# A state space layer in one fused kernel: projection split so that times and angles come first, functions on ScalarE put in order, one scaling moved from GpSimd to ScalarE

## The chip, the cores and the metric

The kernel runs on one core of a Trainium2 chip. A core has five engines that run side by side, each working through its own queue in order: PE (TensorE, matrix products into the PSUM memory), DVE (VectorE, elementwise work and sums along a row), ACT (ScalarE, functions such as exp, tanh, sine, one instruction at a time with a table of functions loaded), POOL (GpSimd, elementwise work from SBUF and scatters by index) and SP (SyncE, which here issues the transfers). The metric is device time in microseconds of a whole execution; smaller is better.

## The reference

Four sequences of 512 tokens, 128 numbers each, go through four layers. Each layer's result is added to its input and the sum is normalised.

1. Attention in a band of 64 tokens to either side, 16 heads.
2. A mixture of experts: 12 experts, of which each token takes the best two, plus one shared expert.
3. A state space layer, cut here to what the change touches:

```python
proj = u @ W_in                                   # 684 columns
z, x, Bp, Cp, dd_dt, dd_A, trap_raw, angles = jnp.split(proj, idx, axis=-1)   # 256 256 64 64 4 4 4 32
Bp = _layernorm(Bp, Bn_g, Bn_b);  Cp = _layernorm(Cp, Cn_g, Cn_b)
DT = jax.nn.softplus(dd_dt + dt_bias)
phase = jnp.cumsum(angles * DT.mean(-1, keepdims=True), axis=1)
Bp_rot, Cp_rot = _rope_pairs(Bp, phase), _rope_pairs(Cp, phase)     # turned by cos and sin of phase
A = jnp.minimum(-jax.nn.softplus(dd_A), -A_FLOOR)
decay = jnp.exp(A * DT);  trap = jax.nn.sigmoid(trap_raw)
# h = decay * h + (trap * x B + (1 - trap) * previous x B) * DT ;  y = h C      step by step
y = (y + D_param * x4) * jax.nn.silu(z4)
out = y @ W_out
```

4. A second mixture of experts: 8 experts of width 512, the best two, each expert's result normalised before it is weighted.

## The kernel before

Tokens lie on the 128 partitions, in four blocks per sequence. The program has three parts.

The first (lines 1698 to 1703) is attention, then routing and the first experts. Tokens are scattered by POOL into a table in main memory, one stretch per expert; tiles of 128 rows are loaded, multiplied, and scattered back (`ys_a`). The third (1716 to 1725) does the same for the second experts. In both, each engine's queue has the order in which the program is written (`as_written`).

The change lies in the second part, lines 1706 to 1715. Two generators `pair(0)` and `pair(1)`, for two sequences each, are traced in turns: pair 0 alone for 40 us of the costs that stand in its `yield` statements, then the two side by side, whichever has had less cost first (`side_by_side`). Within a pair `together` takes one step of each of several generators in turn. Here the order on each engine is not the order of tracing: the framework's planner plays the program through at compile time with durations of its own; an engine takes, of the instructions that are ready in this play, the one traced first. The queue so made is then fixed, and on the chip an instruction that waits holds up all behind it on its engine.

One pair goes through these steps, all in `ssm` (1494):

- `moe0_back` (1058): loads the two results of each token's two experts (`back`, two buffers, on SP's queue), and `combine` (1042) weights them. POOL multiplies the first result by its weight (1046) and adds the shared expert's output (1047); DVE adds the second (1051) and takes mean and variance. `layernorm` then takes a root on ACT (299) and normalises on ACT (312).
- `ssm_project` (1119): transposes the rows on PE and copies them to SBUF on ACT (290, 293). For each of 8 blocks it multiplies by the last 428 columns of the weights (1132) and ACT copies the result to `pj` (1135). Then the first 256 columns, the gate `z`, are projected in transposed form (1141), ACT takes the tanh (1144), and DVE makes `zt` (1147).
- `ssm_norm` (1150) and `ssm_weights` (1178), together. The first squares B and C on ACT (1156), sums on DVE (1159), takes a root on ACT, multiplies on DVE (1165) and applies gain and bias on POOL (1173, four operations). The second works on the 44 columns of times and angles: bias (1187), tanh and exp (1194, 1196), logarithm (1203), a row of small DVE steps to `vals` (1205 to 1227), a shift by one token and a prefix sum on PE (1233 to 1250), range reduction on DVE (1258 to 1264), three sums for decays on PE (1269), sine and cosine (1275, 1277) and exp (1282, 1285) on ACT. The decays are stored as rows in main memory (1308) so that `chunk_load` (1367) can load them spread over the partitions.
- `ssm_turn` (1311): turns B and C by sine and cosine on DVE and POOL (1324, 1325, 1330), transposes them (1342), and forms their products (1359, 1362).
- For each of four blocks, `chunk_matrix` (1385) makes the decay matrix by a scan on DVE (1395) and a product on POOL (1414), and the scaled x on POOL and ACT (1403, 1409). `chunk_outputs` (1424) forms the state and the outputs on PE (1432, 1441, 1447, 1454) and multiplies by `zt` (1472). `chunk_out` (1477) projects out and adds the residual. After two blocks follow the layer norm and the routing for the second experts: gates on DVE, ranks on PE (425), scatters on POOL (467).

Six PSUM banks (`bank`) go round for all products of this part. The tiles `nrm` and the decay matrices share two SBUF buffers (tag `b`).

Of the kernel before, what the change touches and what calls it, by code (L numbers as in the profile page):

```python
# [9 lines left out]
F32 = mybir.dt.float32  # L10
BF16 = mybir.dt.bfloat16
I32 = mybir.dt.int32
AF = mybir.ActivationFunctionType
# [3 lines left out]
P = 128  # L17
# [12 lines left out]
NPROJ = 684  # L30
# [9 lines left out]
class Kernel:  # L40
# [34 lines left out]
    @contextmanager  # L75
    def as_written(self, *engines):

        e = mybir.EngineType
        kinds = {"PE": e.PE, "ACT": e.Activation, "DVE": e.DVE, "POOL": e.Pool, "SP": e.SP}
        last = self.nc.cur_bb.bb.instructions[-1]  # L80
        yield
        traced = self.nc.cur_bb.bb.instructions
        first = next(i for i in reversed(range(len(traced))) if traced[i] is last) + 1
        before = {kinds[k]: [] for k in engines}
        puts = {}
        order = mybir.DependencyInfo(mybir.DependencyClass.NoSync, mybir.DependencyReason.DATA)
        for i in traced[first:]:
            if i.engine in before:
                put = i.name in self.put_names
                for name in before[i.engine] + ([] if put else puts.get(i.engine, [])):  # L90
                    self.tc.add_manual_dep(i, name, order, reason="as written")

                if put:
                    puts.setdefault(i.engine, []).append(i.name)
                else:
                    before[i.engine], puts[i.engine] = [i.name], []

# [944 lines left out]
    def combine(self, y, back, w, mv):  # L1042
# [3 lines left out]
        nc.gpsimd.tensor_tensor(first, first, w[:, 0, :, None].to_broadcast([P, NT, D]), ALU.mult)  # L1046
        nc.gpsimd.tensor_tensor(first, first, y, ALU.add)
        yield 2.6
# [70 lines left out]
    def ssm_project(self, h, x, s):  # L1119


        nc = self.nc
        n = NPROJ - DI
        xt = [self.transposed([x[k][:, i, :] for i in range(NT)], f"xt2_{h}{k}") for k in range(HB)]
        pj = s["pj"] = self.sp.tile([P, HC, n], F32, tag="pj", name=f"pj{h}")
        zt = s["zt"] = self.sp.tile([P, 2, HB, T], F32, tag="zt", name=f"zt{h}")
        yield 1.2
        yield 0.5
        for i in range(NT):
            for k in range(HB):  # L1130
                pp = self.bank(f"ppj{h}_{i}_{k}")
                nc.tensor.matmul(
                    pp[:, :n], lhsT=xt[k][:, i * P : (i + 1) * P], rhs=self.w_in[:, DI:], start=True, stop=True
                )
                nc.scalar.copy(pj[:, i * HB + k, :], pp[:, :n])
            yield 1.6
        for k in range(HB):
            pz = [self.bank(f"pz{h}_{k}_{c}") for c in range(2)]
            tz = [self.s2.tile([P, T], F32, tag="a", name=f"tz{h}_{k}_{c}", bufs=9) for c in range(2)]
            for c in range(2):  # L1140
# [3 lines left out]
                nc.scalar.activation(tz[c], pz[c], AF.Tanh, scale=0.5)  # L1144
# [33 lines left out]
    def ssm_weights(self, h, s):  # L1178

        nc, n = self.nc, HC  # L1180
        o = DI + 2 * NS
        pj = s["pj"]
# [5 lines left out]
            v, pj[:, :, o : o + 8], self.dtb[:, None, :].to_broadcast([P, n, 8]), ALU.add  # L1188
# [5 lines left out]
        nc.scalar.activation(tr, pj[:, :, o + 8 : o + 12], AF.Tanh, scale=0.5)  # L1194
# [33 lines left out]
            vals.rearrange("p (c k) -> p c k", c=n), pj[:, :, o + 12 : o + 44],  # L1228
# [39 lines left out]
        for k, lhsT in enumerate((self.gt, self.ones, self.lt)):  # L1268
# [6 lines left out]
        nc.scalar.activation(sn.rearrange("p c k -> p (c k)"), r, AF.Sin)  # L1275
        cs = self.s2.tile([P, n, 32], F32, tag="c", name=f"cs{h}", bufs=5)
        nc.scalar.activation(
            cs.rearrange("p c k -> p (c k)"), ph, AF.Sin, bias=self.half_pi, scale=-1.0
        )
        s["turn"] = sn, cs  # L1280
        dec = small([P, 4, n, NH1], "dec")
        nc.scalar.activation(
            dec[:, :3].rearrange("p k i h -> p (k i h)"), pd[:, : 3 * m], AF.Exp
        )
        nc.scalar.activation(dec[:, 3], ash, AF.Exp)
# [208 lines left out]
    def ssm(self, h, first, behind):  # L1494
# [5 lines left out]
        yield from self.ssm_project(h, x, s)  # L1500
        yield from self.together([self.ssm_norm(h, s), self.ssm_weights(h, s)])
        for i in range(2):
            self.chunk_load(h, i, s)
        yield from self.ssm_turn(h, s)
# [271 lines left out]
```

## Time and profile before

| | |
|---|---|
| Median of 3 runs | 702.22 us (702.03 to 704.40) |
| The profiled execution, device time | 701.83 us |
| Its span in the trace | 700.1 us |
| Busy: PE, weight load, DVE, ACT, POOL | 510.5, 372.4, 424.2, 307.2, 358.7 us |
| Last scatter of the first experts issued | 373.22 us |
| First loaded rows weighted (line 1046) | 381.63 us |
| First weights step of pair 0 (line 1187) | 404.85 us |
| Sine of pair 0, of pair 1 (line 1275) | 428.44, 473.23 us |
| First scan of pair 0 (line 1395) | 435.92 us |
| First bias copy of the second experts (line 546) | 570.97 us |

How to read the profile: times are us from the start of the span, and the span is some 1.7 us shorter than the device time. A line of the timeline gives start, length, engine, line, operation, output<-input with partitions x elements, and in brackets how long the engine sat idle before and what ended the wait. "PEld" is the load of a stationary operand. A float32 product appears as two matmul passes. An average over the span says little here, since its parts have different limits; the stretches are read one by one.

### The profile page before, as it was taken

Reading aid. Unit: us, or ns where it says so; the run is one execution under the profiler, and the core shown is the slowest. Engines: PE = TensorE matmul, PEld = TensorE weight load, DVE = VectorE, ACT = ScalarE, POOL = GpSimd, SP = SyncE. Lnnn points to the kernel's source line nnn. Section 1 sums busy time; section 2 is a strip of 40 time slices with the busy share of each in tenths; the row PEclk is TensorE's granted clock in tenths of the full one; section 3 lists DMA queues with packets and bytes.
Section 4 is the critical chain, followed back from the end, with each engine's and each line's share of the span. In section 5 each row is a group of like instructions: output and inputs, shape, how many; then the busy total and the mean of one; then the engine's idle time right before and its main releaser. Section 6 shows DMA issues by size and latency. Waiting matters only on the chain.

```text
span 700.1 us, 13358 instructions
## 1 busy us (share of the span) xinstructions
PE 510.5 (73%) x4232; PEld 372.4 (53%) x4232; DVE 424.2 (61%) x1412; ACT 307.2 (44%) x799; POOL 358.7 (51%) x509
## 2 busy tenths in 40 slices
PE   6899789688886985999992618673675569898800
PEld 2344344254443644999992306363464459888700
DVE  5565656756734361566662666999774535777745
ACT  2154554454462420455551474914423317566525
POOL 9254324723847041455554322667864655888831
PEclk9799999979978696899997676766676559999955
DMA  6999999998000004688876202113110135766442
GB/s 177 220 158 154 160 157 155 154 143 125 32 2 31 1 23 143 176 249 250 256 220 183 74 0 84 46 38 107 45 47 16 46 84 156 187 179 179 125 133 60
DMA packets 93936, 83.63 MB, mean 119 GB/s; under 512 B 8869, under 2 KB 78650, under 8 KB 93866
## 3 DMA queue, kind: packets, MB, share of 16 engines
q1 hardware_dynamic: 88554, 71.85, 48.0%
q0 software_dynamic: 5312, 10.92, 5.3%
q8 instruction: 35, 0.57, 0.3%
q14 instruction: 35, 0.29, 0.1%
HBM read 50.54 MB, written 32.20 MB: 118 GB/s over the span
## 4 chain that ended last, share of the span: by engine, by line
PE 48%; DVE 21%; ACT 10%; DMA 9%; POOL 6%; issue 5%; SPq 1%; POOLq 0%; ACTq 0%; DVEq 0%
PE pa L1023 4%; PE pg L1023 4%; PE pse L803 4%; DMA io_b<-table_b 4%; PE psc L773 4%; PE py_a L575 3%; ACT pt L807 3%; PE ph L1600 3%; PE pc L826 3%; PE psc L766 2%; PE py_b L575 2%; DVE maxima L779 2%; POOL table_a L467 2%; PE pys L1002 2%; DMA ys_b<-io_b,at_b 2%
## 5 line engine op out<-in xcount | busy, mean ns | idle before, releaser
L811 POOL TENSOR_SCALAR_AFFINE_SELECT pt<-pt 128x1024 f32<-128x1024 f32 (+1 forms) x64 | 61.5, 985 | 93.9 <-ACT pt L807 87.6
L779 DVE TENSOR_REDUCE maxima<-psc 128x2 f32<-128x384 f32 x128 | 62.4, 550 | 45.9 <-PE psc L773 45.9
L807 ACT ACTIVATE pt<-pse 128x384 f32<-128x384 f32 (+1 forms) x128 | 59.2, 550 | 63.1 <-PE pse L803 63.1
L467 POOL DMA_INDIRECT ys_a<-io_a,at_a x43 | 42.1, 978 | 49.8 <-DVE at_a L566 49.5
L1032 DVE SCALAR_TENSOR_TENSOR act<-pa,bias_a,ge 128x128 f32<-128x128 f32 x129 | 37.4, 345 | 49.4 <-ACT ge L1031 29.5
L1603 ACT ACTIVATE hid<-ph,bias_b 128x128 f32<-128x128 f32 x156 | 44.6, 369 | 24.0 <-PE ph L1600 20.8
L766 PE MATMUL psc<-band,ident_bf 128*64 128x384 bf16 (+1 forms) x192 | 39.1, 349 | 12.5 <-ACT pt L807 7.5
L1031 ACT ACTIVATE ge<-pg,bias_a 128x128 f32<-128x128 f32 x129 | 38.1, 366 | 21.4 <-DVE at_a L566 16.8
L467 POOL DMA_INDIRECT table_a<-x,put x32 | 31.9, 996 | 24.6 <-DVE e_cnt L454 13.0
L1600 PE MATMUL ph<-io_b,wt_b 128*128 128x128 f32 x312 | 43.2, 283 | 0.0
L467 POOL DMA_INDIRECT ys_b<-io_b,at_b x39 | 39.0, 1001 | 7.6 <-issue 5.8
L575 PE MATMUL py_b<-down,hid 128*128 x312 | 41.8, 277 | 0.8 <-DVE io_b L1610 0.7
L467 POOL DMA_INDIRECT table_b<-r,put x32 | 31.8, 994 | 20.5 <-issue 7.9
L803 PE MATMUL pse<-q,k 32*128 32x256 f32 (+1 forms) x512 | 40.8, 398 | 1.8 <-DVE q L789 1.8
L1600 PEld LDWEIGHTS ph<-io_b,wt_b 128*128 128x128 f32 x312 | 39.5, 198 | 0.0
L575 PEld LDWEIGHTS py_b<-down,hid 128*128 128x128 f32 x312 | 38.3, 193 | 1.2 <-ACT hid L1603 1.0
L1023 PE MATMUL pg<-io_a,wt_a 128*128 128x128 f32 x258 | 37.2, 282 | 0.0
L1023 PE MATMUL pa<-io_a,wt_a 128*128 128x128 f32 x258 | 37.1, 282 | 0.0
L803 PEld LDWEIGHTS pse<-q,k 32*128 32x128 f32 x512 | 28.9, 202 | 15.1 <-issue 6.8
L575 PE MATMUL py_a<-down,act 128*128 x258 | 36.4, 278 | 0.0
L826 PE MATMUL pc<-pt,v 128*32 128x256 f32 (+1 forms) x512 | 34.1, 389 | 0.6 <-POOL pt L811 0.6
L1023 PEld LDWEIGHTS pa<-io_a,wt_a 128*128 128x128 f32 x258 | 33.6, 199 | 0.0
(340 smaller groups left out, 1219.1 us busy)
## 6 DMA issues: line engine op xcount, KB each, us to landing
wt_a<-in_We_dram SPq DMA_DIRECT2D x43, 384.0 KB
table_a<-zero SPq DMA_DIRECT2D x12, 1040.0 KB
wt_b<-in_w_dram SPq DMA_DIRECT2D x39, 256.0 KB
table_b<-zero SPq DMA_DIRECT2D x8, 1040.0 KB
dbc<-rows SPq DMA_DIRECT2D x8, 512.0 KB
io_a<-table_a SPq DMA_DIRECT2D x43, 65.0 KB
io_b<-table_b SPq DMA_DIRECT2D x39, 65.0 KB
down<-in_We_dram SPq DMA_DIRECT2D x12, 192.0 KB
```

The lines of the kernel that those rows point to most:

```text
L467: put = self.nc.gpsimd.indirect_dma_start(out=out, out_offset=bass.IndirectOffsetOnAxis(ap=at, axis=0), in_=x, in_offset=None)
L575: nc.tensor.matmul(py[:, :D], lhsT=hidden[:, c * P : (c + 1) * P], rhs=flat[:, bass.ds(r["reg"][t, 2] + c * D, D)], start=c == 0, stop=c = ...
L766: nc.tensor.matmul(pp[part], lhsT=self.ident_bf[:, part], rhs=self.band[:, None, off : off + w].to_broadcast([P, 2, w]), start=True, stop= ...
L779: nc.vector.tensor_reduce(self.maxima[b % 2][:, j, at : at + 2], pp, AX.X, ALU.max)
L803: nc.tensor.matmul(pp[:, c], lhsT=s["k"][strip, 2 * cp + c, m * P : (m + 1) * P], rhs=s["q"][strip, c, lo:hi], start=True, stop=True, skip ...
L807: nc.scalar.activation(pt[:, 2 * i : 2 * i + 2, :w], pp, AF.Exp)
L811: nc.gpsimd.affine_select(out=x, in_=x, compare_op=ALU.is_ge, fill=0.0, base=HALF if m == 0 and sign > 0 else 0, pattern=[[0, 2 * G], [sig ...
L826: nc.tensor.matmul(acc[32 * i : 32 * i + 32, lo:hi], lhsT=s["v"][:, m, 4 * i + 2 * cp + c, :], rhs=pt[:, 2 * i + c, : hi - lo], start=m == ...
L1023: nc.tensor.matmul(p[:, c * P : (c + 1) * P], lhsT=wt[:, at : at + P], rhs=xt, start=True, stop=True,)
L1031: nc.scalar.activation(ge[:, cb], pg[:, cb], AF.Gelu, bias=bias[:, 3 + c : 4 + c])
L1600: nc.tensor.matmul(ph[:, cb], lhsT=s["wt"][:, cb], rhs=s["xt"], start=True, stop=True)
L1603: nc.scalar.activation(hid[:, cb], ph[:, cb], AF.Gelu, bias=s["bias"][:, c : c + 1])
```

## The change

Five edits, all in the second part or in what it calls.

- A helper `behind(x, y)` makes the planner put one instruction after another on its engine, with no wait on the chip. With it sine comes after both exp, cosine after sine, and the gate's tanh after cosine.
- The 44 columns of times and angles are projected first, by a generator of their own, into one PSUM bank, and the weights read them there. The other projection has 384 columns instead of 428.
- The weights start together with this projection, and the norm follows it, instead of both starting after it.
- The gate (`ssm_gate`) is traced together with the turn, instead of within the projection.
- In `combine` ACT scales the first result, block by block, and POOL adds two blocks at a time. The `yield` after it says 2.0 instead of 2.6.

```diff
-NPROJ = 684
+NPROJ, TIMES = 684, 640
+    def behind(self, x, y):
+        order = mybir.DependencyInfo(mybir.DependencyClass.NoSync, mybir.DependencyReason.DATA)
+        self.tc.add_manual_dep(x.ins, y.ins.name, order, reason="as written")
...
         first = back[:, :, 1, :D]
-        nc.gpsimd.tensor_tensor(first, first, w[:, 0, :, None].to_broadcast([P, NT, D]), ALU.mult)
-        nc.gpsimd.tensor_tensor(first, first, y, ALU.add)
-        yield 2.6
+        for i in range(NT):
+            nc.scalar.activation(first[:, i, :], first[:, i, :], AF.Copy, scale=w[:, 0, i : i + 1])
+            if i % 2:
+                part = slice(i - 1, i + 1)
+                nc.gpsimd.tensor_tensor(first[:, part], first[:, part], y[:, part], ALU.add)
+        yield 2.0
...
-    def ssm_project(self, h, x, s):
-        nc = self.nc
-        n = NPROJ - DI
-        xt = [self.transposed([x[k][:, i, :] for i in range(NT)], f"xt2_{h}{k}") for k in range(HB)]
+    def ssm_times(self, h, x, s):
+        nc, n = self.nc, NPROJ - TIMES
+        xt = s["xt"] = [self.transposed([x[k][:, i, :] for i in range(NT)], f"xt2_{h}{k}") for k in range(HB)]
+        yield 1.7
+        pt = self.bank(f"ptimes{h}")[:, : HC * n]
+        s["times"] = pt.rearrange("p (c n) -> p c n", c=HC)
+        for i in range(NT):
+            for k in range(HB):
+                c = i * HB + k
+                nc.tensor.matmul(
+                    pt[:, c * n : (c + 1) * n], lhsT=xt[k][:, i * P : (i + 1) * P], rhs=self.w_in[:, TIMES:],
+                    start=True, stop=True,
+                )
+        yield 1.0
+
+    def ssm_project(self, h, s):
+        nc = self.nc
+        xt, n = s["xt"], TIMES - DI
         pj = s["pj"] = self.sp.tile([P, HC, n], F32, tag="pj", name=f"pj{h}")
-        zt = s["zt"] = self.sp.tile([P, 2, HB, T], F32, tag="zt", name=f"zt{h}")
-        yield 1.2
-        yield 0.5
...
-                    pp[:, :n], lhsT=xt[k][:, i * P : (i + 1) * P], rhs=self.w_in[:, DI:], start=True, stop=True
+                    pp[:, :n], lhsT=xt[k][:, i * P : (i + 1) * P], rhs=self.w_in[:, DI:TIMES], start=True, stop=True
                 )
                 nc.scalar.copy(pj[:, i * HB + k, :], pp[:, :n])
             yield 1.6
+        yield from self.ssm_norm(h, s)
+
+    def ssm_gate(self, h, s):
+        nc = self.nc
+        xt = s.pop("xt")
+        zt = s["zt"] = self.sp.tile([P, 2, HB, T], F32, tag="zt", name=f"zt{h}")
         for k in range(HB):
...
-                nc.scalar.activation(tz[c], pz[c], AF.Tanh, scale=0.5)
+                i = nc.scalar.activation(tz[c], pz[c], AF.Tanh, scale=0.5)
+                self.behind(i, s["sines"])
...
     def ssm_weights(self, h, s):
-        o = DI + 2 * NS
-        pj = s["pj"]
+        times = s.pop("times")
-            v, pj[:, :, o : o + 8], self.dtb[:, None, :].to_broadcast([P, n, 8]), ALU.add
+            v, times[:, :, :8], self.dtb[:, None, :].to_broadcast([P, n, 8]), ALU.add
-        nc.scalar.activation(tr, pj[:, :, o + 8 : o + 12], AF.Tanh, scale=0.5)
+        nc.scalar.activation(tr, times[:, :, 8:12], AF.Tanh, scale=0.5)
-            vals.rearrange("p (c k) -> p c k", c=n), pj[:, :, o + 12 : o + 44],
+            vals.rearrange("p (c k) -> p c k", c=n), times[:, :, 12:44],
...
-        nc.scalar.activation(sn.rearrange("p c k -> p (c k)"), r, AF.Sin)
+        sines = nc.scalar.activation(sn.rearrange("p c k -> p (c k)"), r, AF.Sin)
-        nc.scalar.activation(
+        s["sines"] = nc.scalar.activation(
             cs.rearrange("p c k -> p (c k)"), ph, AF.Sin, bias=self.half_pi, scale=-1.0
         )
+        self.behind(s["sines"], sines)
-        nc.scalar.activation(
-            dec[:, :3].rearrange("p k i h -> p (k i h)"), pd[:, : 3 * m], AF.Exp
-        )
-        nc.scalar.activation(dec[:, 3], ash, AF.Exp)
+        for i in (
+            nc.scalar.activation(dec[:, 3], ash, AF.Exp),
+            nc.scalar.activation(dec[:, :3].rearrange("p k i h -> p (k i h)"), pd[:, : 3 * m], AF.Exp),
+        ):
+            self.behind(sines, i)
...
-        yield from self.ssm_project(h, x, s)
-        yield from self.together([self.ssm_norm(h, s), self.ssm_weights(h, s)])
+        yield from self.ssm_times(h, x, s)
+        yield from self.together([self.ssm_project(h, s), self.ssm_weights(h, s)])
         for i in range(2):
             self.chunk_load(h, i, s)
-        yield from self.ssm_turn(h, s)
+        yield from self.together([self.ssm_turn(h, s), self.ssm_gate(h, s)])
```

## The prediction

> **What bounds the kernel now.** I first read the mean per stretch, to find where the change lies. The state space layer of both pairs runs from the last scatter of the first experts (373 us) to the first bias copy of the second experts (571 us). Table of stretches: start and end, length, busy us (and instructions) of PE, weight load, DVE, ACT, POOL, then PE clock, DMA share, GB/s.
>
> ```profile
> 391.00:405.00 14.00, 13.93 (x32) 6.26 (x32) 6.79 (x29) 9.55 (x25) 4.42 (x4) 0.81 0.13 37
> 405.00:420.00 15.00, 0.63 (x3) 0.66 (x4) 11.51 (x22) 9.93 (x16) 5.23 (x4) 0.67 0.00 0
> 420.00:436.00 16.00, 13.52 (x44) 9.80 (x44) 9.52 (x25) 6.75 (x13) 4.64 (x5) 0.61 0.32 92
> 436.00:450.00 14.00, 11.19 (x56) 5.92 (x54) 12.34 (x20) 12.12 (x25) 6.24 (x5) 0.87 0.16 47
> 450.00:470.00 20.00, 11.89 (x74) 9.78 (x73) 18.47 (x32) 6.42 (x20) 16.60 (x16) 0.55 0.08 29
> 470.00:490.00 20.00, 8.81 (x81) 7.21 (x80) 19.86 (x41) 9.14 (x24) 14.28 (x12) 0.71 0.32 105
> ```
>
> Until 436 no engine is full throughout: a chain of small steps of the first pair sets the pace, and between 405 and 420 TensorE does 0.63 us. From 450 to 490 DVE is busy 38.33 of 40 us. So the earlier stretch has time to give, and the later one passes it on only if its own work doesn't grow.
>
> Second, the timeline of ACT, which links the steps of that chain (start, length, then what; in brackets the idle time before it and its releaser).
>
> ```profile
> 399.11 0.30 ACT L299 ACTIVATE rstd<-mv,eps 128x4 f32<-128x4 f32 x1 [4.36 <-DVE mv L319]
> ...
> 405.22 1.28 ACT L1144 ACT_TABLE_LOAD   x1
> 406.52 2.07 ACT L1144 ACTIVATE tz<-pz 128x512 f32<-128x512 f32 x4
> 408.44 1.08 ACT L1156 ACTIVATE nrm<-pj 128x1024 f32<-128x1024 f32 x1
> 409.39 0.25 ACT L1194 ACTIVATE trap<-pj 128x32 f32<-128x32 f32 x1
> 409.51 0.27 ACT L1196 ACTIVATE sp_e<-sp_e 128x64 f32<-128x64 f32 x1
> ...
> 412.18 1.28 ACT L1203 ACT_TABLE_LOAD   x1
> 413.48 0.26 ACT L1203 ACTIVATE sp_l<-sp_u 128x64 f32<-128x64 f32 x1
> ...
> 428.44 0.42 ACT L1275 ACTIVATE sn<-phr 128x256 f32<-128x256 f32 x1
> ```
>
> The first line is the second pair's root, standing in ACT's queue before the first pair's copies of the projection: 4.36 us lost. The small tanh and exp stand behind four gate tanh (`tz`) and the square. Sine comes at 428.44. Third, DVE and POOL:
>
> ```profile
> 404.85 0.22 DVE L1187 TENSOR_TENSOR sp_v<-pj,dtb 128x64 f32<-128x64 f32 x1 [4.02 <-ACT pj L1135]
> ...
> 415.01 1.30 DVE L1208 TENSOR_TENSOR sp_l<-sp_l,sp_u 128x64 f32<-128x64 f32 x1
> ```
>
> ```profile
> 381.63 1.04 POOL L1046 TENSOR_TENSOR back_a<-back_a,gw 128x512 f32<-128x512 f32 x1 [7.45 <-DMA back_a<-ys_a]
> ...
> 414.98 1.26 POOL L1173 TENSOR_TENSOR nrm<-nrm,bcb 128x512 f32<-128x512 f32 x1
> ```
>
> The weights' first step (404.85) waits for the eighth copy of all 428 columns, of which it needs 44. The subtraction at 415.01 takes 1.30 us for 64 columns, beside a POOL operation; the same step's neighbours without POOL take 0.2.
>
> **The change, part by part.** Times are of the profiled execution, in us from the start of the span.
>
> Scaling on ACT. Before, POOL does multiply and add for two sequences from 381.63 to 386.18. The second experts' end has the new form already: four scalings of 128x128 on ACT in 1.28, and two POOL adds of 128x256 in 1.41 to 1.68. So the adds run from about 382.3 to 385.2: 1.0 earlier. DVE's combinations (1.2 each beside POOL, 0.31 alone) start 0.8 earlier and end 1.0 earlier. ACT is idle until 389.25, which hides these eight scalings; without that cover they would cost 2.6. The second pair's rows are loaded on SP's queue when the first pair's buffers are free (387.44), so they too come about 1 earlier and land at about 390.3. Its own eight scalings (2.6) fall among the first pair's eight normalisings (3.19) and two copies (1.25) on ACT: what is queued behind them is the transposed copy, and behind that all the projection. If the planner puts them ahead before the rows have landed, it costs 0 to 2; I take 0.5. Net gain at the start of the projection: 0.5.
>
> Times first. The projection starts at 393.6 instead of 394.13. 16 passes (8 blocks, two per matmul) of 44 columns: nearest row, eight transposes of 128 columns in 1.91, that is 0.24 a pass; 3.8 in all (bounds 3.1 by the weight load of 0.191, 6.4 by 0.4). So the first weights step can run at 397.5, and beside the second pair's statistics on DVE at 398.0. It gains 6.9.
>
> From there to sine: 23.6 before. After: two DVE steps 0.5; table and tanh and exp 1.7; DVE 0.2; table and logarithm 1.6; ten small DVE steps at the free pace of 0.2 (POOL has no work then, its normalisation comes later) 2.2, before 5.6; angles times step 0.4; the two prefix sums on TensorE 3.4 plus 0.5 behind a projection pass; range reduction 3.5 (3.3 in the second pair, 4.2 in the first). That is 14.0. On ACT stand between them the projection copies (eight at 0.5, now 384 columns, overlapping to some 3.0), the second pair's two roots and eight normalisings (0.6 and 3.2), the square, its root and further tables. Bounds: 0 if all falls into gaps, 8 if all stands ahead. I take 4.5, so sine at 416.5 instead of 428.44: 11.9 earlier. The two exp of the decays now stand before sine by order, where they stood anyway; cost nothing.
>
> Is ACT itself the limit? From 393.6 to 416.5 it has scalings 2.6, transposed copies 1.2, roots 0.9, normalisings 3.2, projection copies 3.0, square 1.0, small functions 1.2 and six table loads. By the row a load takes 1.28 and the next instruction starts 0.02 later (405.22 to 406.52): 7.8, sum 20.9 of 22.9. The Trainium skill, page "ScalarE: Activation LUTs", section "What ACT_TABLE_LOAD costs", counts 1.28 for the load and 1.38 more for a drain, 2.66 per switch: then 29.1, sine at 422.7 at the earliest and, with the same slack, at 424.7: only 3.7 of the 11.9 are left. The trace has no such gap, so I keep the row; but ACT is close to full.
>
> The other branch. The 384-column projection follows the times at 397.4 and ends at 404.1 (16 passes at 0.42, scaled from 428 columns in 7.44 for 16); copy 0.5, square 1.1, sum 1.2, table and root 1.6, two DVE products 1.3, four POOL operations of 1.3 each: 415.0. It meets sine almost exactly, so the rotation starts at 417 at the latest instead of 428.96: 12.0 gained, and the first pair's transposes at 421.6 instead of 433.65.
>
> Gate moved behind the cosine. Four tanh (2.07) and a table load leave the chain; they come after 417 while ACT waits for the transposes (before, idle 2.55 there), so part is covered. The four DVE products (2.48) move from an empty place (407) to the threshold of the full stretch: cost 2.5. If ACT had no gap, the copies of `bt` and `ct` would wait up to 3.4 more. Their first reader is the output product of the first chunk (456 before), so nothing waits for them otherwise.
>
> The loads on SP follow the weights: the store of the rows (426.25 before) and the chunk's loads behind it (428.12), whose data the first scan had by 435.92, so 7.8 after issue at most. 12 earlier these are 416.1 and 423.9; the first scan is due at 426.4, so they stay hidden.
>
> PSUM. One of six banks is held by the times until the angles are read. The projection's copies keep pace with five: at most one pass, 0.5, cost 0 taken.
>
> Sum: 12.0 - 2.5 = 9.5 at the start of the chunks. DVE is then the bound, with unchanged work, so its stretch moves as a whole; the second pair's own weights come earlier too (its times no longer wait for its copies), which I count as nothing. 701.8 - 9.5 = 692.3 against the profiled 701.83 (span 700.1 and 1.7 around it); the median of the runs lies 0.4 higher: 692.7.
>
> **The rivals.** (1) Absorbed: what sets the end is the second pair, whose rotation waits at 475 for DVE. For it: DVE at 96% from 450 to 490, and its store of rows stands on SP's queue behind the first pair's chunk loads, which wait for output products up to 14.7 us. Against: DVE idles 10.0 of the 31 us from 405 to 436, and this idle time is what is filled. If half of the gain is lost to new waits there: 697.5. (2) No effect: the planner orders queues from its own durations and again puts the second pair's root ahead of the small tanh, and the late second pair's chain blocks both; then 5 of the 11.9 are gone, the gate takes 2.5, and the other 4.4 are lost in the full stretch as in (1): 702. (3) Slower: TensorE's in-order queue in the tail. Rank products of the routing already hold it up, waiting for DVE:
>
> ```profile
> PE prank_b L425 <- DVE rh L414: 17.2, 4, 7.8
> ```
>
> Four waits, 17.2 us, the longest 7.8, with chunk outputs queued behind them. All order between 373 and 571 is planned anew, so rank products may stand before more chunk outputs. Two more such waits of 7.8 on the path cost 15.6 and give 708; it decides from 9.5 on. Against: nothing in the edit touches the routing. (4) More: the second pair's rotation comes earlier in the order too, frees its `nrm` buffer, and the chunks' matrices, which share these two buffers, need not wait for one another: the scans at 449.37 and 465.75 are 16 apart. I give it 8 more: 684.
>
> **How the numbers follow.** Likeliest case 0.50 (692.7, own range 687 to 698), absorbed 0.17, no effect 0.08, slower 0.17, more 0.08. The range 685 to 704 leaves out about half of the slower case and half of the last, with some tail. 0.5% (3.5 us) is about what a measurement of this kernel can tell from no change. Faster: 0.50 + 0.08 + 0.14 of the absorbed = 0.72; within: 0.11; slower: 0.17.
>
> **What would show it.** First weights step near 398, sine near 416, first scan near 426 (435.92 before), first bias copy of the second experts near 561.5. Wrong if ACT waits before the small tanh again, if sine is later than 422, or if the stretch from the second pair's rotation (478.4) to that bias copy, now 92.6 us, grows.

## The result, and the profile after

The changed kernel takes 696.41 us (median of 4 runs, 694.51 to 697.46) where the kernel before took 702.12 beside it (701.9 to 704.4): ratio 0.9908, 95% interval 0.9879 to 0.9938. The gain of the medians is 5.7 us; 9.5 were forecast. The profiled execution took 697.46 us (span 695.8, granted clock 0.83), 4.4 less than the 701.83 of before. Some executions run in a slower state: all ratios leave these out, and where a profile below is of a slow one (scaling alone; no second gate product, where 12 of 22 executions were slow; `yt` first with the own buffer), only distances within it are read.

All times below are us from the start of the span, and line numbers are those of each version's own kernel. Where kernels are compared, they are counted from the **landing**: the first use of the first experts' rows, 381.63 before and 382.94 after. Ahead of it the engines run the same instructions in the same order in both programs, so its 1.3 us are scatter. From the landing to the first bias copy of the second experts: 570.97 - 381.63 = 189.3 before, 565.52 - 382.94 = 182.6 after. That is 6.7 less. The landing takes back 1.3, and from the bias copy to the end of the span stand 130.3 instead of 129.1: 6.7 - 1.3 - 1.2 = 4.2, against 4.3 between the spans.

The stretches of the changed kernel (start and end, length, busy us and instructions of PE, weight load, DVE, ACT, POOL, then PE clock, DMA share, GB/s):

```profile
391.00:405.00 14.00, 13.52 (x36) 8.77 (x37) 2.30 (x12) 9.28 (x23) 1.37 (x2) 0.53 0.09 31
405.00:420.00 15.00, 9.28 (x28) 5.57 (x26) 10.74 (x31) 10.78 (x19) 5.54 (x5) 0.77 0.00 0
420.00:436.00 16.00, 8.68 (x34) 5.56 (x35) 14.28 (x36) 10.26 (x21) 11.38 (x11) 0.68 0.34 100
436.00:450.00 14.00, 10.59 (x80) 7.77 (x78) 10.11 (x29) 12.99 (x33) 4.48 (x4) 1.00 0.14 39
450.00:470.00 20.00, 11.32 (x74) 7.18 (x75) 18.47 (x41) 7.33 (x16) 15.70 (x15) 0.74 0.20 68
470.00:490.00 20.00, 9.29 (x86) 6.33 (x86) 18.84 (x23) 9.20 (x27) 17.67 (x12) 0.73 0.18 66
```

TensorE now has 9.28 us of work between 405 and 420 instead of 0.63, so the empty stretch is filled. But DVE went from 9.52 to 14.28 us between 420 and 436, where the first pair's rotation was to run free; and from 450 to 490 it is still busy 37.31 of 40.

The chain to sine, in the timeline of ACT after:

```profile
397.84 1.28 ACT L1220 ACT_TABLE_LOAD   x1
399.86 0.20 ACT L1220 ACTIVATE trap<-ptimes 128x32 f32<-128x32 f32 x1 [0.74 <-DVE sp_v L1213]
...
406.41 1.28 ACT L1229 ACT_TABLE_LOAD   x1
407.71 0.26 ACT L1229 ACTIVATE sp_l<-sp_u 128x64 f32<-128x64 f32 x1
407.87 0.46 ACT L1154 COPY pj<-ppj 128x384 f32<-128x384 f32 x1
408.23 0.40 ACT L1052 ACTIVATE back_a<-back_a,gw 128x128 f32<-128x128 f32 x1
408.53 1.04 ACT L1183 ACTIVATE nrm<-pj 128x1024 f32<-128x1024 f32 x1
409.48 0.68 ACT L1052 ACTIVATE back_a<-back_a,gw 128x128 f32<-128x128 f32 x2
...
417.57 0.42 ACT L1301 ACTIVATE sn<-phr 128x256 f32<-128x256 f32 x1 [1.84 <-DVE phr L1289]
419.05 0.51 ACT L1303 ACTIVATE cs<-ph,half_pi 128x256 f32<-128x256 f32 x1 [1.06 <-DVE ph L1290]
```

The small tanh no longer stands behind a root or four gate tanh. Sine comes 34.6 after the landing instead of 46.8: 12.2 gained, 11.9 forecast. Two lines are to be kept in mind: the second pair's scalings (`back_a`) stand at 408.23 and 409.48, in the midst of the first pair's chain.

POOL and DVE between the functions (cosine done at 419.6) and the rotation (`rt`):

```profile
415.74 1.65 POOL L1200 TENSOR_TENSOR nrm<-nrm,bcg 128x512 f32<-128x512 f32 x1 [4.82 <-DVE nrm L1192]
...
420.22 1.26 POOL L1200 TENSOR_TENSOR nrm<-nrm,bcb 128x512 f32<-128x512 f32 x1
421.44 1.48 POOL L1353 TENSOR_TENSOR rt<-nrm,sn 128x256 f32<-128x256 f32 x2
```

```profile
419.21 1.08 DVE L1059 SCALAR_TENSOR_TENSOR y<-back_a,gw 128x128 f32<-128x128 f32 x1
420.21 0.17 DVE L324 BATCH_NORM_AGGREGATE mv<-st 128x2 f32<-128x6 f32 x1
420.30 1.32 DVE L1059 SCALAR_TENSOR_TENSOR y<-back_a,gw 128x128 f32<-128x128 f32 x1
...
424.71 0.76 DVE L1352 TENSOR_TENSOR rt<-nrm,cs 128x256 f32<-128x256 f32 x2
...
464.76 0.75 DVE L1500 TENSOR_TENSOR yt<-py,zt 128x256 f32<-128x256 f32 x2
...
471.57 1.31 DVE L1352 TENSOR_TENSOR rt<-nrm,sn 128x256 f32<-128x256 f32 x2 [0.16 <-PE py L1469]
472.80 1.29 DVE L1358 TENSOR_TENSOR rot<-rt 128x256 f32<-128x256 f32 x2
```

The other branch, B and C with their norm, is ready only at 421.48. Then DVE still has the second pair's statistics and the first pair's decay weights in front of the rotation, 3.2 us, with the second pair's combinations just ahead of them. The rotation's start on DVE gained 5.5 (47.3 to 41.8 after the landing), not 12.0. And on PE the first pair keeps none of it:

```profile
427.32 2.01 PE L295 MATMUL tp_xt<-ident,y 128*128 128x128 f32 x5 [9.15 <-ACT y L317]
...
436.74 1.04 PE L1370 MATMUL pbc<-ident,rot 128*128 128x128 f32 x8
```

Its rotated rows are done at 427.76, but in PE's queue the second pair's rows (`tp_xt`) and projection stand ahead of its transposes (`pbc`), and those rows kept PE waiting 9.15 us. The transposes come 53.8 after the landing; before it was 52.0.

The last lines of DVE above belong to the second pair: the second half of its rotation starts when PE has begun an output product (`py`) of the first. PE at that place:

```profile
465.32 2.04 PE L1511 MATMUL pso<-w_W_out,yt 128*128 128x128 f32 x8 [7.57 <-DVE yt L1500]
467.16 2.84 PE L1167 MATMUL pz<-xt,w_W_in 128*128 128x512 f32 x4
469.93 0.65 PE L1460 MATMUL pst<-xs,rot 128*64 128x256 f32 x4
470.41 1.04 PE L1469 MATMUL py<-m,xw 128*64 128x128 f32 x16
471.38 1.16 PE L1475 MATMUL py<-ident,xo 128*128 128x128 f32 x8
472.47 0.67 PE L1482 MATMUL py<-ubc,state 64*64 64x128 f32 x16
473.81 1.09 PE L1370 MATMUL pbc<-ident,rot 128*128 128x128 f32 x8 [0.67 <-DVE rot L1358]
```

PE waits 7.57 us for the gated output of the first pair's second chunk (`yt`); behind that wait stand the out-projection, the gate's products, the third chunk's output products, and only then the second pair's transposes (`pbc`). In the kernel before those output products began at 472.38 and the transposes at 479.20, after this wait:

```profile
474.44 0.67 PE L1454 MATMUL py<-ubc,state 64*64 64x128 f32 x16
479.20 1.97 PE L1342 MATMUL pbc<-ident,rot 128*128 128x128 f32 x8 [4.09 <-DVE rot L1330]
```

So before, the second pair's turn was late for its own reason, sine at 473.23. Afterwards its sine comes at 456.34, 18.2 earlier from the landing, yet its transposes only 6.7 (97.6 to 90.9): the turn has run up against the first pair's third chunk. From the transposes to the bias copy 91.8 and 91.7 us pass (570.97 - 479.20 and 565.52 - 473.81): in these two profiles the end moves with the second pair's turn.

Why is `yt` late? PE had finished its last input at 454.43 (first line), and the gate factor `zt` of the first pair is older still. DVE reached it at 464.76, 10.3 us later. Meanwhile DVE worked without a gap (second line, in the form of the table of stretches: DVE busy 17.45 of 17.55 us) at the second pair's range reduction, decay weights and half a rotation, and at the first pair's next scans:

```profile
453.76 0.67 PE L1482 MATMUL py<-ubc,state 64*64 64x128 f32 x16
```

```profile
449.15:466.70 17.55, 8.54 (x69) 6.21 (x70) 17.45 (x35) 7.35 (x17) 16.40 (x15) 0.78 0.19 63
```

The routing's rank products, rival 3, did not grow (total wait, times, longest):

```profile
PE prank_b L430 <- DVE rh L419: 16.2, 4, 6.5
```

### The profile page after: what moved, and what is told of

The parts are those of the page before. It is cut to its first block, busy times and chain, and to the rows that moved or that the text cites. A ratio compares the mean times of both kernels' runs of the same rounds, so it can differ in the third digit from the quotient of the medians.

```text
span 695.8 us, 13449 instructions
## 1 busy us (share of the span) xinstructions
PE 511.5 (74%) x4264; PEld 374.2 (54%) x4264; DVE 417.3 (60%) x1412; ACT 313.4 (45%) x816; POOL 357.3 (51%) x509
## 5 line engine op out<-in xcount | busy, mean ns | idle before, releaser
L816 POOL TENSOR_SCALAR_AFFINE_SELECT pt<-pt 128x1024 f32<-128x1024 f32 (+1 forms) x64 | 61.6, 987 | 95.4 <-ACT pt L812 89.1
L580 PE MATMUL py_b<-down,hid 128*128 x312 | 41.8, 277 | 0.3
L1028 PEld LDWEIGHTS pa<-io_a,wt_a 128*128 128x128 f32 x258 | 33.6, 199 | 0.0
```

The source lines that it names most:

```text
L580: nc.tensor.matmul(py[:, :D], lhsT=hidden[:, c * P : (c + 1) * P], rhs=flat[:, bass.ds(r["reg"][t, 2] + c * D, D)], start=c == 0, stop=c = ...
L816: nc.gpsimd.affine_select(out=x, in_=x, compare_op=ALU.is_ge, fill=0.0, base=HALF if m == 0 and sign > 0 else 0, pattern=[[0, 2 * G], [sig ...
L1028: nc.tensor.matmul(p[:, c * P : (c + 1) * P], lhsT=wt[:, at : at + P], rhs=xt, start=True, stop=True,)
```

## The experiments

The experiments ran on other chips, where the kernel before took 714.8, 713.7, 713.7 and 702.8 us and executions of one kernel scatter by 1 to 2%; so ratios to the kernel before on the same chip are given, and for anything under 3 us the landmarks counted from the landing. Up to the second pair's transposes these repeat within 0.2 us between two executions of the changed kernel, the bias copy only within 2.5. The changed kernel itself ran again on the second of these chips alone; elsewhere its ratio is compared across chips.

**First theory: the second pair's scalings.** They stand last on ACT, so its combination falls in front of the first pair's rotation. If that is what cost the missing 4 to 5 us, scaling on GpSimd gives them back.

All scaling on GpSimd, the rest as changed:

```diff
-        for i in range(NT):
-            nc.scalar.activation(first[:, i, :], first[:, i, :], AF.Copy, scale=w[:, 0, i : i + 1])
...
+        nc.gpsimd.tensor_tensor(first, first, w[:, 0, :, None].to_broadcast([P, NT, D]), ALU.mult)
+        nc.gpsimd.tensor_tensor(first, first, y, ALU.add)
...
```

> The changed kernel with the scaling of the first result left on POOL for all four sequences. Theory: the scalings of the second pair string out on ACT (the last ends at 410), so its combination reaches DVE at 413 to 422, in front of the first pair's rotation, and its rows are normalised so late (427) that TensorE's queue holds the first pair's transposes until 436.7. On POOL this combination ends near 400, the first pair's transposes come at 425 to 428, and the time is 688 to 693 us, though the first pair starts 1 us later. Rival: the rotation is late because DVE runs beside POOL's normalisation (415.7 to 421.4), whoever scales: transposes after 433, and 696.5 to 699 us.

Measured: 0.9906 (0.9870 to 0.9941), not to be told from the change. The first pair's rotation does start 5.5 earlier (36.3 after the landing) and its transposes 5.6 earlier (48.2 instead of 53.8), but the second pair's transposes come at 90.4 instead of 90.9.

Only the first pair scaled on ACT:

```diff
+        if b < HB:
             for i in range(NT):
                 nc.scalar.activation(first[:, i, :], first[:, i, :], AF.Copy, scale=w[:, 0, i : i + 1])
...
+        else:
+            nc.gpsimd.tensor_tensor(first, first, w[:, 0, :, None].to_broadcast([P, NT, D]), ALU.mult)
...
```

> The changed kernel, scaling on ACT for the first pair and on POOL for the second. Theory: as with all on POOL, and the first pair keeps its head start of 1 us: 687 to 692 us, second pair's combination done on DVE near 399. Rival (late rotation comes from POOL's normalisation beside DVE): 696 to 697.5 us, as the changed kernel.

Measured: 0.9903 (0.9867 to 0.9940). The first pair's rotation starts 7.3 earlier (34.5), the second pair's transposes 3.1 earlier (87.8), the bias copy at 180.6. A gain of 2 or 3 us would not show in the ratio. The theory falls: the 5.5 and 7.3 us given back to the first pair bring the second pair's transposes forward by no more than 0.5 and 3.1.

**The parts of the change.** The scaling alone, put into the kernel before (the edit of the change, nothing else):

> The kernel before, with only the scaling moved to ACT. Theory: the first pair's head start of 1 us is given back by the second pair's scalings among the first pair's copies: 701 to 704 us, sine of the first pair within 2 us of before. Rival: it is the scaling that gave the gain: 695 to 698 us.

Measured: 0.9962 (0.9942 to 0.9981), so 2.7 us of 714.8, where the forecast had 0.5. In the profile, sine of the first pair comes 44.1 after its landing instead of 46.8. Since the changed kernel without the scaling is at 0.9906, no gain on top of the other edits shows, with intervals of some 2.5 us to either side.

The gate back in the projection, the rest as changed:

```diff
             yield 1.6
+        yield from self.ssm_gate(h, s)
         yield from self.ssm_norm(h, s)
...
-                i = nc.scalar.activation(tz[c], pz[c], AF.Tanh, scale=0.5)
-                self.behind(i, s["sines"])
+                nc.scalar.activation(tz[c], pz[c], AF.Tanh, scale=0.5)
...
-        yield from self.together([self.ssm_turn(h, s), self.ssm_gate(h, s)])
+        yield from self.ssm_turn(h, s)
```

> The changed kernel with the gate back in the projection: its four tanh are traced and run before the norm, not behind the cosine. Theory: moving the gate is worth the four tanh (2.1 us) on ACT at most, most of which falls into ACT's waits for TensorE: 695 to 699 us, sine of the first pair at 417 to 420. Rival: the gate out of the chain is what carries the gain: 700 to 703 us, sine after 422.

Measured: 0.9941 (0.9917 to 0.9965) where the change has 0.9908: 0.0033 x 714.8 = 2.4 us slower, with intervals that overlap. The landmarks are clearer: the bias copy comes at 190.6, against 182.6 and 185.1 in two executions of the changed kernel. The first pair's sine is not later for it (33.6 after the landing), so the gate's tanh was not what held sine. The loss is in the second pair: transposes at 95.2 instead of 90.9. PE of this version, at the same place as above:

```profile
477.24 1.22 PE L1511 MATMUL pso<-w_W_out,yt 128*128 128x128 f32 x4 [10.67 <-DVE yt L1500]
```

It is the same wait for `yt`, 10.67 us long instead of 7.57; `yt` comes at 86.1 instead of 81.8.

**Second round: what holds the second pair's turn.** Three answers. A: its rotation's second half shares two buffers (tag `b`) with `nrm` and the chunks' matrices, and must wait for an output product to free one. B: the PE queue, with the transposes behind the first pair's output work, which waits for `yt`. C: DVE is full (37.31 of 40 us), so order moves nothing. The changed kernel ran again beside these three:

> The changed kernel itself, as the measure for the other three on the same chip. Ratio to the kernel before 0.991 (0.988 to 0.994 was measured first). From the landing of the first experts' rows to the first bias copy 182.6 us, second pair's transposes 90.9 after the landing, from there to the bias copy 91.7.

Measured: 0.9884 (0.9846 to 0.9921); transposes at 91.1, bias copy at 185.1 (182.6 in the first profile: the stretch behind the transposes alone differs by 2.3 between two executions).

A buffer of its own for the rotation's second half:

```diff
-            t = self.s2.tile([P, 2, 2] + shape[1:], F32, tag="tb"[half], name=f"rt{h}_{half}", bufs=1 + half)
+            t = self.s2.tile([P, 2, 2] + shape[1:], F32, tag="tq"[half], name=f"rt{h}_{half}", bufs=1)
```

> The second half of the rotation gets a buffer of its own, so it no longer waits for an output product of the first pair. Theory A (the shared buffer is the wait that holds the second pair's rotation): the second half starts at 80 to 82 after the landing instead of 88.6, its transposes at 84 to 86 instead of 90.9, total 5 us less than the changed kernel. Theory B (TensorE's in-order queue holds it: the second pair's transposes stand behind output work of the first pair that waits for a late product on VectorE): the rotation is done earlier, but the transposes stay at 89 to 91 and the total gains at most 1 us. Theory C (VectorE is full from 450 to 490 us, order moves nothing): rotation and total within 1 us.

Measured: 0.9865 (0.9823 to 0.9907). The later half of the rotation starts at 84.0 instead of 88.6, but the transposes at 92.4, straight behind the output products. The rotated rows were done 3.0 us before that, so here PE's queue alone held the transposes. A falls as the sole cause.

`yt` ordered ahead of the second pair's decay weights:

```diff
-        nc.vector.tensor_tensor(w[:, 0], dec[:, 3], wa, ALU.mult)
+        x = nc.vector.tensor_tensor(w[:, 0], dec[:, 3], wa, ALU.mult)
+        if h == 1:
+            self.late.append(x)
+            for t in self.yts:
+                self.behind(x, t)
...
```

> VectorE makes the gated output of the first pair's second chunk before the second pair's decay weights; the rotation's second half still shares its buffer. Theory A (buffer): that half waits for the output products behind the gated output, which come 2 to 4 us earlier, so total 2 to 4 us less. Theory B (TensorE's queue): the same, 2 to 4 us less, since the transposes stand behind the same work. Theory C (VectorE full): within 1 us of the changed kernel, with the same 91.7 us from the transposes to the bias copy.

Measured: 0.9871 (0.9832 to 0.9909), transposes at 92.0. It tells nothing: `yt` is at 82.4, not earlier; the copies of the decays and the first half of the rotation still stand ahead of it, and took 3.6 us instead of 2.3.

Both edits:

> Both edits: the buffer of its own and the gated output earlier. Theory A (buffer): as with the buffer alone, 5 us less than the changed kernel. Theory B (TensorE's queue): more than either alone, 3 to 6 us less, the transposes of the second pair at 85 to 88 after the landing. Theory C (VectorE full): within 1 us; if the transposes do come earlier, the stretch from them to the bias copy grows by as much.

Measured: 0.9842 (0.9807 to 0.9877), medians 3.8 below the changed kernel on the same chip (702.37 and 706.20; the intervals overlap). `yt` 81.7, transposes 90.2, bias copy 180.6. The transposes hardly moved, so B's figure of 85 to 88 was missed. What did move is DVE's work behind the rotation: the next chunk's scan starts at 89.8 instead of 91.3. That this carries the rest of the gain is argued, not shown.

Then work was taken from DVE at this place, to test C. The second pair's gate products are left out, so its gate is the tanh alone:

```diff
+                if h == 0:
                     nc.vector.scalar_tensor_tensor(zt[:, c, k, :], tz[c], 1.0, pz[c], ALU.add, ALU.mult)
...
```

> The changed kernel, leaving out the second pair's gate products (x times the half of 1 + tanh): its gate is the tanh alone. VectorE has four operations of 0.65 us less, 2.6 in all, between 471 and 479 us. Theory C (VectorE's full queue sets the second pair's turn and the end): the transposes of the second pair and the end come 2 to 2.6 us earlier, ratio about 0.985. Theory B (a wait holds the turn: its second half for its buffer, its transposes for output work ahead on TensorE): VectorE idles in their place, transposes at 90 to 91 as before, total within 1 us of the changed kernel, ratio 0.988 to 0.991.

Measured: 0.9879 (0.9842 to 0.9915), as the changed kernel. Its DVE and PE:

```profile
480.15 0.42 DVE L1495 TENSOR_TENSOR state<-pst,state 128x256 f32<-128x256 f32 x1 [1.55 <-PE pst L1461]
481.10 1.30 DVE L1353 TENSOR_TENSOR rt<-nrm,sn 128x256 f32<-128x256 f32 x2 [0.52 <-PE py L1470]
```

```profile
474.89 2.05 PE L1512 MATMUL pso<-w_W_out,yt 128*128 128x128 f32 x8 [7.59 <-DVE yt L1501]
...
483.33 1.09 PE L1371 MATMUL pbc<-ident,rot 128*128 128x128 f32 x8 [0.67 <-DVE rot L1359]
```

Its landing is at 392.44: the later half of the rotation at 88.7, transposes at 90.9, both within 0.1 of the changed kernel. With 2.6 us less to do, DVE stands idle 1.55 and 0.52 for PE instead. So DVE's work between `yt` and the transposes does not set the turn. About DVE's work ahead of `yt` this version says nothing, since the products left out stand behind it; in the changed kernel, where `yt` starts at 464.76:

```profile
465.43 1.28 DVE L1174 SCALAR_TENSOR_TENSOR zt<-tz,pz 128x512 f32<-128x512 f32 x2
...
469.80 0.69 DVE L1174 SCALAR_TENSOR_TENSOR zt<-tz,pz 128x512 f32<-128x512 f32 x1 [0.72 <-ACT tz L1170]
470.72 0.69 DVE L1174 SCALAR_TENSOR_TENSOR zt<-tz,pz 128x512 f32<-128x512 f32 x1 [0.23 <-ACT tz L1170]
```

`yt` itself is late because it stands behind 10 us of other DVE work, so DVE's queue does take part, by its order.

`yt` ahead of the weights, the decays' copies and the rotation's first half (each put behind it as the weights were), with the own buffer:

```diff
-            nc.vector.tensor_copy(all_[part], dec[part, 1, k::HB, :])
+            x = nc.vector.tensor_copy(all_[part], dec[part, 1, k::HB, :])
...
-                nc.vector.tensor_tensor(t[:, 0, g], nrm[:, :, g, :, 0::2], first, ALU.mult)
+                x = nc.vector.tensor_tensor(t[:, 0, g], nrm[:, :, g, :, 0::2], first, ALU.mult)
...
```

> VectorE makes the gated output of the first pair's second chunk before the second pair's decay weights, the copies of its decays and the first half of its rotation; the rotation's second half has a buffer of its own. In the version with the weights alone behind it the product did not move (81.7 after the landing, 81.9 in the changed kernel). Theory B (TensorE's queue holds the second pair's transposes behind output work that waits for this product): the product comes at 77 to 78, the transposes at 86 to 88 instead of 90.2, total 2 to 4 us less than the version with both edits, ratio to the kernel before 0.979 to 0.982. Theory C (VectorE is full, order moves nothing): transposes may move, but the bias copy stays at 180 to 183 after the landing, ratio 0.984 to 0.988.

Measured: 0.9817 (0.9762 to 0.9872). `yt` came 2.2 earlier than in the changed kernel (79.6), the transposes only 0.5 (90.4): the third chunk's output products now waited 1.10 for the second pair's gate products, which free their PSUM bank. Each wait that is taken out of this queue is followed by the next.

The same, with the second pair's scaling on GpSimd as in the run further up, twice:

> The same, and the second pair's first results are scaled on GpSimd as before. Landing to bias copy was 2 us shorter with that split alone than in the changed kernel (180.6 against 182.6). Theory B: both add up, transposes of the second pair at 83 to 86 after the landing, bias copy at 176 to 178, ratio 0.976 to 0.980. Theory C: no better than 180, ratio 0.984 or more.

> The version with the gated output first, the rotation's own buffer and the second pair's scaling on GpSimd, once more, to see whether its ratio holds: 0.982 was measured with an interval of 0.977 to 0.987, against 0.991 and 0.988 for the changed kernel in two measurements. Theory B (the second pair's turn is what the end follows, and these edits bring it 4 us nearer): 0.979 to 0.985, bias copy at 177 to 179 after the landing. Theory C (order moves nothing, the earlier figure was chance): 0.987 to 0.992.

Measured: 0.9819 (0.9769 to 0.9868) and 0.9807 (0.9760 to 0.9854), the latter 687.46 us against 702.83. This is the lowest ratio of the study, though not clear of the 0.9817 just before. Transposes at 87.0 in both, bias copy at 177.6 and 176.0. PE of the second:

```profile
458.52 1.45 PE L1533 MATMUL pso<-w_W_out,yt 128*128 128x128 f32 x8 [2.31 <-DVE yt L1518]
459.75 3.29 PE L1173 MATMUL pz<-xt,w_W_in 128*128 128x512 f32 x4
462.98 0.65 PE L1478 MATMUL pst<-xs,rot 128*64 128x256 f32 x4
463.46 1.04 PE L1487 MATMUL py<-m,xw 128*64 128x128 f32 x16
464.43 1.16 PE L1493 MATMUL py<-ident,xo 128*128 128x128 f32 x8
465.52 0.67 PE L1500 MATMUL py<-ubc,state 64*64 64x128 f32 x16
466.12 1.10 PE L1388 MATMUL pbc<-ident,rot 128*128 128x128 f32 x8
```

The wait for `yt` is 2.31 instead of 7.57, and nothing waits behind it. Not all of this is due to the order: with the scaling split alone (the version with only the first pair scaled on ACT) `yt` came at 78.9 already, and PE waited

```profile
471.64 2.05 PE L1516 MATMUL pso<-w_W_out,yt 128*128 128x128 f32 x8 [2.71 <-DVE yt L1505]
```

That C in its strict form, order moves nothing, falls is shown here. DVE is busy 125.4 us between the landing and the bias copy in this version and 126.0 in the one with the own buffer alone, which has the same DVE instructions in another order, and the bias copy comes at 176.0 and 183.0.

The table puts all of it side by side, us after the landing (`yt`: start of its DVE products, of the second one where the two stand apart (scaling alone, gate as before); later half: third of the four DVE products of the second pair's rotation; third output: end of the first pair's third output products on PE):

| | Sine, pair 1 | `yt` | Third output ends | Rotation, later half | Transposes, pair 1 | Bias copy | Ratio |
|---|---|---|---|---|---|---|---|
| Before | 91.6 | 86.9 | 93.5 | 95.8 | 97.6 | 189.3 | 1 |
| Scaling alone | 90.2 | 83.0 | 94.4 | 94.1 | 96.4 | 188.5 | 0.9962 |
| Changed | 73.4 | 81.8 | 90.2 | 88.6 | 90.9 | 182.6 | 0.9908 |
| Changed, again | 73.5 | 81.9 | 90.4 | 88.8 | 91.1 | 185.1 | 0.9884 |
| Scaling on GpSimd | 74.7 | 81.6 | 89.7 | 88.1 | 90.4 | 183.1 | 0.9906 |
| First pair on ACT | 71.9 | 78.9 | 87.1 | 85.5 | 87.8 | 180.6 | 0.9903 |
| Gate as before | 75.8 | 86.1 | 93.8 | 92.2 | 95.2 | 190.6 | 0.9941 |
| Own buffer | 74.9 | 83.4 | 92.5 | 84.0 | 92.4 | 183.0 | 0.9865 |
| `yt` ahead of weights | 74.0 | 82.4 | 91.4 | 89.8 | 92.0 | 185.5 | 0.9871 |
| Both | 73.4 | 81.7 | 90.2 | 83.2 | 90.2 | 180.6 | 0.9842 |
| No second gate product | 73.4 | 81.9 | 90.2 | 88.7 | 90.9 | 183.9 | 0.9879 |
| `yt` first, own buffer | 74.9 | 79.6 | 90.4 | 84.9 | 90.4 | 183.0 | 0.9817 |
| The same, scaling split | 72.8 | 79.0 | 87.0 | 83.1 | 87.0 | 177.6 | 0.9819 |
| The same again | 71.9 | 78.8 | 87.1 | 83.0 | 87.0 | 176.0 | 0.9807 |

In every version that projects times first, the second pair's sine is ready at 72 to 76, and its transposes begin within 1.4 us of the end of the third output products. Where the buffer is shared they still wait for the rotation, by 0.67 to 1.35, since its later half starts only behind an output product; with the own buffer they come with the end of the output products. Before, and with the scaling alone, they came 4.1 and 2.0 after it, waiting for the rotation.

## Why the prediction was right, and where not

The time came out inside the likeliest case's own range (687 to 698), and the head of the change, up to sine, did what the working said. From there on the gain took another way than forecast, so that 5.7 lies as near to 9.5 as it does is in part luck: the first pair's gain was lost again at its transposes, and what reached the end came by the second pair, which the working counted as nothing.

- **Times first**: forecast 398.0 for the first weights step, measured 399.60, of which 1.3 is the landing. Right.
- **Sine**: 14.0 of steps and 4.5 of ACT queueing forecast, in sum 11.9 gained; 12.2 measured. Right. The Trainium skill, page "ScalarE: Activation LUTs", section "What ACT_TABLE_LOAD costs", would, by the estimate made from its 2.66 us a switch, have let only 3.7 of it through. The trace after has 1.28 and then 0.02 (406.41 to 407.71), as the row before had; the row was the right choice.
- **The other branch** was to leave the rotation at 417 "at the latest", and so 12.0 gained. This is the step that failed first. The norm ended at 421.48 instead of 415.0: the projection's last copy came behind a table load and the logarithm (407.87), the reciprocal waited on DVE from the root at 412.0 to 414.55, and POOL's four operations took 5.7 instead of 5.2; 1.3 is the landing. Then 3.2 went to DVE's queue. The working had the second pair's scalings on ACT cost "0 to 2; I take 0.5" and looked only at what is queued behind them on ACT. It did not follow their readers: POOL's adds at 408.76 and 410.23, then DVE's combinations up to 421.6, among the first pair's range reduction and ahead of its rotation. With the second pair's scaling on GpSimd again, the rotation starts 5.5 to 7.3 earlier. The first pair's transposes, forecast at 421.6, came at 436.74: the working had no term for PE's queue, where the second pair's rows and projection stood ahead of them. The first scan came at 430.72, 6.5 earlier from the landing; the chunk's loads, which were to stay hidden, held it up for 1.53 at the end.
- **Gate**: a cost of 2.5 was forecast. With the gate left in place the ratio is 0.9941 against 0.9908, and the second pair's transposes come 4.3 later: moving it gains, by an amount that the overlapping intervals leave open. The four products did go into a fuller stretch, but with the gate where it was the wait for `yt` is longer. The sign was wrong.
- **Scaling**: 0.5 forecast, 2.7 measured alone, none seen on top of the rest.
- **The sum**: "12.0 - 2.5 = 9.5 at the start of the chunks. DVE is then the bound, with unchanged work, so its stretch moves as a whole". Half of it stands: the stretch from the second pair's rotation to the bias copy did not grow (from the last product of the rotation, 570.97 - 479.07 = 91.9 before and 565.52 - 473.68 = 91.8 after). But it does not start with the first pair's chunks, and DVE's work is not unchanged: from the landing to the bias copy DVE is busy 126.8 us instead of 134.4, with as many instructions. The stretch starts with the second pair's turn, whose earlier weights "I count as nothing". That turn gained 6.7: 3.3 because the first pair's third output ends earlier (93.5 to 90.2), and 3.4 because the second pair's rotation, waited for 4.09 before, is now waited for 0.67. The mis-sized term is this one: 9.5 was to be 6.7.
- **Rival 1** said that what sets the end is the second pair, whose rotation waits, and gave 697.5. In mechanism and in size it is closer to what was found than the likeliest case. Of its reasons, the busy DVE is half right: it holds up not the rotation but `yt`, for which PE waits, with the second pair's transposes behind it. The other hold is the shared buffer. The store of the rows on SP's queue shows in no wait there.

Left open:

- How much the buffer, the order and the scaling split each count in the fastest version. Ratios and landmarks disagree on it: with `yt` first and the own buffer the ratio is 0.9817 and the bias copy stands at 183.0; with the split alone these are 0.9903 and 180.6.
- Why the distance from the transposes to the bias copy varies from 88.9 to 95.4 between versions, and by 2.3 between two executions of the changed kernel.
- What part of the second pair's 6.7 is due to TensorE's granted clock: from 450 to 470 it was 0.74 in the changed kernel's profile and 0.55 before, and no run separates it.
- A version that puts the second pair's transposes ahead of the third output on PE was not tried. In the fastest version the rotated rows are done only 0.4 us before PE reaches the transposes, so this order alone could gain no more there.

## What to carry to other kernels

When two chains run side by side, forecast the one that the end follows: ask of each gain which wait of the *later* chain ends last once its own inputs are early, and read that from the queue ahead of it on the engine where the two meet. A busy share of 93% does not say which of an engine's work sets the end. Find the product for which another engine waits: work left out behind it changed nothing here, while the work ahead of it made it 10 us late. So leave out or move work ahead of that product, and see whether the landmark moves. A step moved to another engine must be followed to its last reader, since what it delays may be on a third engine: here scalings on ACT, combinations on DVE and at last row transposes on PE, ahead of the first pair's.

## What the runs showed of the hardware

The same clamp of 128x256 on DVE (the last but one step of the range reduction) took 1.14 to 1.36 us where POOL's operations of 128x512 ran beside it and 0.27 to 0.29 with POOL idle, in different versions of one kernel. So moving POOL's normalisation in time changes DVE's chain without an instruction more. In the changed kernel the first pair's range reduction has two operations stretched so (416.18 and 417.73, 1.36 and 1.29 us long, against 0.29 and 0.43 before), beside POOL's of 415.74 to 418.7: some 1.9 us. The forecast knew the effect, but had POOL's work end at 415.0, where it ended at 421.48.
